# Two stacked graph layers on one core: the order of the weight loads, the place of the bias products, and when the second graph's values are made

## The chip, the cores and the metric

One core of one Trainium2 chip runs the whole program. The metric is the device time of one execution in microseconds (us). Medians of separate sets are given with the number of runs. Instruction times come from one profiled execution of each kernel; the span of a profile is about 1.8 us below the time of that same execution.

## The reference, cut to what matters

64 graphs of 256 nodes and 256 features pass two layers. All arithmetic is fp32.

```python
# layer 0: two graph attention (GAT) steps, then a feed-forward (FF) block
h = gat(gat(x, adj, W1, a1), adj, W2, a2)
h = layernorm(x + h, g_ln1, b_ln1)
x = layernorm(h + relu(h @ w_ff1 + b_ff1) @ w_ff2 + b_ff2, g_ln2, b_ln2)
# layer 1: relational attention of 8 heads, then an FF block with gelu
q, k = x @ Wq + bq, x @ Wk + bk
out = sum over r of (softmax(q k') * (adj == r)) @ (x @ Wv[r] + bv[r])
x = layernorm(x + out @ Wo + bo, g1, beta1)
x = layernorm(x + gelu(x @ W1 + b1) @ W2 + b2, g2, beta2)
```

All biases of the test inputs are zero; the kernels compute with them all the same.

## The kernel before

Graphs go in 32 pairs. Each pair is a generator of steps ("way"), and up to three ways run interleaved, so that TensorE (PE) has work of one pair while another waits.

The biases b_ff2, bo and b2 would have to be added to rows of 256 columns. The kernel adds each to the beta of the layer norm ahead of it instead, and corrects the next layer's bias for it by a tiny product: bias - W' b. These are products with a single moving column. Before any pair starts, a setup block makes them all:

```python
loaded = {0: load(0)}                     # xT, adjT, x of pair 0: first in the queue
...                                       # W1T, a2, W2, a1c; then w12 = W1 @ [W2, ...] on PE
ln = ...                                  # eight rows for the layer norms
ff0, wq, wk, wo, wv, bq, bk, bv, ff1 = ...  # all weights
with tc.tile_pool(name="psetup", bufs=2, space=PSUM) as psetup:
    for n, (name, readers) in enumerate((("L0_gnn_b_ff2", ((ff0[0], ff0[1]),)),
                                         ("L1_gnn_bo", ((wq, bq), (wk, bk))),
                                         ("L1_gnn_b2", ((ff1[0], ff1[1]),)))):
        ...                               # loads the bias row and the bias column here
        for w, bias in readers:
            pw = psetup.tile([P, 512], F32, name="pw")
            for m in range(w.shape[-1] // P):
                for c in range(KC):
                    nc.tensor.matmul(pw[:, m:m + 1], lhsT=w[:, c, m * P:(m + 1) * P], rhs=b[:, c:c + 1], ...)
            nc.vector.tensor_tensor(bias, bias, pw[:, :of], ALU.subtract)
        ...                               # for bo also one wide product with wv
psum = tc.tile_pool(name="psum", bufs=8, space=PSUM)   # the banks that the pairs' products go to
```

A pair's way, and the attention loop in it (two graphs b, two groups c of four heads each):

```python
def whole_way(pair):
    yield from gat_layers(pair, xT, adjT, x)   # inside: loaded[pair + 1] = load(pair + 1)
    yield from feed_forward(x, ff0, AF.Relu, ln[1])
    yield from attention(x, pair, adjT)
    yield from feed_forward(x, ff1, AF.Gelu, ln[3])
    ...                                        # store

for n, (b, c) in enumerate(groups):            # in attention
    ...                                        # scores of the next group, products of this one
    if (b, c) == (0, KC - 1):                  # behind the second group: values of graph 1
        v = values_tile()
        for jc in range(2):
            values(v, jc, N + jc * P, yT)
            yield 1.72, 0.0, None
```

xT has a single buffer, adjT and x have four. An fp32 product is two instructions on PE: the 8 products of a pair's first step are x16 in the trace. The second half of the printed kernel, any_inputs, is a general version behind a check of the inputs; no line shown here is from it.

Of the kernel before, what the change touches and what calls it, by code (L numbers as in the profile page):

```python
# [10 lines left out]
F32 = mybir.dt.float32  # L11
# [4 lines left out]
ALU = mybir.AluOpType  # L16
AX = mybir.AxisListType

P = 128
# [10 lines left out]
def two_layers(ctx: ExitStack, tc: tile.TileContext, t: dict, out: bass.AP, flag: bass.AP):  # L30
# [9 lines left out]
    nc = tc.nc  # L40
    B, N, D = out.shape
    NPAIR = B // 2
    KC = D // P
# [6 lines left out]
    SCALE = 1.0 / math.sqrt(DH)  # L50
    assert N == 256 and D == 256 and R == 4

    const = ctx.enter_context(tc.tile_pool(name="const", bufs=1))
    io = ctx.enter_context(tc.tile_pool(name="io", bufs=1))

    def load(pair):
        rows = slice(2 * pair, 2 * pair + 2)
        xT = io.tile([P, KC, 512], F32, name="xT")
        nc.sync.dma_start(xT, t["xT"][pair].rearrange("(c p) b n -> p c (b n)", p=P))
        adjT = io.tile([P, 4, N], I32, name="adjT", bufs=4)  # L60
        nc.sync.dma_start(adjT, t["adjT"][rows].rearrange("b (c p) n -> p (b c) n", p=P))
        x = io.tile([P, 4, D], F32, name="x", bufs=4)
        nc.sync.dma_start(x, t["x"][rows].rearrange("b (c p) d -> p (b c) d", p=P))
        return xT, adjT, x

    loaded = {0: load(0)}


    ident = const.tile([P, P], F32, name="ident")
    make_identity(nc, ident)  # L70
# [10 lines left out]
    def weights(name, pool=const):  # L81
        w = t[name]
        kc, m = w.shape[0] // P, w.shape[1]
        s = pool.tile([P, kc, m], F32, name="w_" + name)
        nc.sync.dma_start(s, w.rearrange("(c p) m -> p c m", p=P))
        return s

    def on_all(name, n, pool=const):

        v = t[name]  # L90
        s = pool.tile([P, n], F32, name="b_" + name)
        nc.sync.dma_start(s, bass.AP(tensor=v.tensor, offset=v.offset, ap=[[0, P], [1, n]]))
        return s

    def column(name):

        s = const.tile([P, t[name].shape[1]], F32, name="c_" + name)
        nc.sync.dma_start(s, t[name])
        return s
# [4 lines left out]
    with tc.tile_pool(name="setup", bufs=1) as setup, \  # L104
            tc.tile_pool(name="psetup", bufs=2, space=bass.MemoryType.PSUM) as psetup:
        w1T, a2 = weights("L0_gnn_W1T", setup), on_all("L0_gnn_a2", 2 * D, setup)
        right = setup.tile([P, KC, D + 4], F32, name="right")
        nc.sync.dma_start(right[:, :, :D], t["L0_gnn_W2"].rearrange("(c p) m -> p c m", p=P))
        nc.sync.dma_start(right[:, :, D + 2:], t["L0_gnn_a1c"])
        junk = setup.tile([P, D], F32, name="junk")  # L110
        for s in range(2):
            for c in range(KC):
                nc.vector.scalar_tensor_tensor(
                    junk, right[:, c, :D], 1.0, a2[:, s * D:(s + 1) * D], op0=ALU.mult, op1=ALU.mult,
                    accum_out=right[:, c, D + s:D + s + 1])
        for m in range(KC):
            pw = psetup.tile([P, 512], F32, name="pw")
            for c in range(KC):
                nc.tensor.matmul(pw[:, :D + 4], lhsT=w1T[:, c, m * P:(m + 1) * P], rhs=right[:, c],
                                 start=c == 0, stop=c == KC - 1)  # L120
            nc.vector.tensor_copy(w12[:, m], pw[:, :D + 4])


    ln = [tuple(on_all(n, D) for n in names) for names in (
        ("L0_gnn_g_ln1", "L0_gnn_b_ln1"), ("L0_gnn_g_ln2", "L0_gnn_b_ln2"),
        ("L1_gnn_g1", "L1_gnn_beta1"), ("L1_gnn_g2", "L1_gnn_beta2"))]
    ff0 = (weights("L0_gnn_w_ff1"), column("L0_gnn_b_ff1"), weights("L0_gnn_w_ff2"))
    wq, wk, wo = weights("L1_gnn_Wq"), weights("L1_gnn_Wk"), weights("L1_gnn_Wo")
    wv = const.tile([P, KC, 2, D], F32, name="wv")
    for c in range(KC):  # L130
        nc.sync.dma_start(wv[:, c], t["L1_gnn_Wv"][:2, c * P:(c + 1) * P, :].rearrange("r p m -> p r m"))
        nc.vector.tensor_tensor(wv[:, c, 1], wv[:, c, 1], wv[:, c, 0], ALU.subtract)
    bq, bk, bv = column("L1_gnn_bq"), column("L1_gnn_bk"), on_all("L1_gnn_bv", 2 * D)
    nc.vector.tensor_tensor(bv[:, D:], bv[:, D:], bv[:, :D], ALU.subtract)
    ff1 = (weights("L1_gnn_W1"), column("L1_gnn_b1"), weights("L1_gnn_W2"))
    bqs = const.tile([P, KC], F32, name="bqs")
    with tc.tile_pool(name="setup", bufs=1) as setup, \
            tc.tile_pool(name="psetup", bufs=2, space=bass.MemoryType.PSUM) as psetup:
        for n, (name, readers) in enumerate((("L0_gnn_b_ff2", ((ff0[0], ff0[1]),)),
                                             ("L1_gnn_bo", ((wq, bq), (wk, bk))),  # L140
                                             ("L1_gnn_b2", ((ff1[0], ff1[1]),)))):
            beta = ln[n][1]
            nc.vector.tensor_tensor(beta, beta, on_all(name, D, setup), ALU.add)
            b = setup.tile([P, KC], F32, name="c_" + name)
            nc.sync.dma_start(b, t[name + "c"])
            for w, bias in readers:
                pw = psetup.tile([P, 512], F32, name="pw")
                of = w.shape[-1] // P
                for m in range(of):
                    for c in range(KC):  # L150
                        nc.tensor.matmul(pw[:, m:m + 1], lhsT=w[:, c, m * P:(m + 1) * P], rhs=b[:, c:c + 1],
                                         start=c == 0, stop=c == KC - 1)
                nc.vector.tensor_tensor(bias, bias, pw[:, :of], ALU.subtract)
            if name == "L1_gnn_bo":
                pw = psetup.tile([P, 512], F32, name="pw")
                for c in range(KC):
                    nc.tensor.matmul(pw, lhsT=b[:, c:c + 1].to_broadcast([P, P]),
                                     rhs=wv[:, c].rearrange("p r m -> p (r m)"), start=c == 0, stop=c == KC - 1)
                nc.vector.tensor_tensor(bv, bv, pw, ALU.subtract)
        nc.vector.tensor_scalar(bqs, bq, SCALE, None, ALU.mult)  # L160

    work = ctx.enter_context(tc.tile_pool(name="work", bufs=1))
    small = ctx.enter_context(tc.tile_pool(name="small", bufs=6))
# [1 line left out]

    def bank():
        return psum.tile([P, 512], F32, name="ps")



# [119 lines left out]
        nc.vector.tensor_tensor(rows, p, rows, ALU.add)  # L290

    def layernorm(r, gb, b):
        g, beta = gb
        st, mv = small.tile([P, 2, 6], F32, name="st"), small.tile([P, 2, 2], F32, name="mv")
        rstd = small.tile([P, 2], F32, name="rstd")
        for j in range(2):
            nc.vector.bn_stats(st[:, j, :], r[:, 2 * b + j, :])  # L297
            nc.vector.bn_aggr(mv[:, j, :], st[:, j, :])
        nc.vector.tensor_scalar(rstd, mv[:, :, 1], EPS, None, ALU.add)  # L299
        nc.gpsimd.tensor_tensor(rstd, rstd, mhalf[:, :2], ALU.pow)  # L300
        for j in range(2):
            row = r[:, 2 * b + j, :]
            nc.vector.scalar_tensor_tensor(row, row, mv[:, j, 0:1], g, op0=ALU.subtract, op1=ALU.mult)
        for j in range(2):
            row = r[:, 2 * b + j, :]
            nc.vector.scalar_tensor_tensor(row, row, rstd[:, j:j + 1], beta, op0=ALU.mult, op1=ALU.add)
# [58 lines left out]
    def attention(y, pair, adjT):  # L365
# [5 lines left out]
        def values_tile():  # L371
            return work.tile([P, 2, 2 * D], F32, name="v", bufs=2)
# [71 lines left out]
        for n, (b, c) in enumerate(groups):  # L444
            last = n == len(groups) - 1
            if not last:
                ahead = scores(*groups[n + 1])
            po = bank()
            sums(e, po)
            products(c, 0, v, e, po)  # L450
            products(c, 1, v, ms, po)
            if not last:
                e, ms = ahead, of_relation_1(groups[n + 1][0], ahead)
            divided(b, c, po)
            yield 3.1 if last else 4.1, 4.8 if last else 0.8, None
            if (b, c) == (0, KC - 1):
                v = values_tile()
                for jc in range(2):
                    values(v, jc, N + jc * P, yT)
                    yield 1.72, 0.0, None  # L460
            if n == 2:
                into_rows(0)
                yield 1.75, 0.0, None
# [4 lines left out]
    def whole_way(pair):  # L468
        yield 0.0, 0.0, "gat"
        xT, adjT, x = loaded.pop(pair)  # L470
        yield from gat_layers(pair, xT, adjT, x)
        yield from feed_forward(x, ff0, AF.Relu, ln[1])
        yield 3.44, 6.0, None
        yield from attention(x, pair, adjT)
        yield from feed_forward(x, ff1, AF.Gelu, ln[3])
        nc.sync.dma_start(out[2 * pair:2 * pair + 2].rearrange("b (c p) d -> p (b c) d", p=P), x)
        yield 3.44, 0.0, None
# [442 lines left out]
```

## Time and profile before

| | before |
|---|---|
| median of the 3 runs at hand for the prediction | 3408.89 us (3407.56 to 3410.56) |
| profiled span | 3408.2 us |
| PE busy | 3341.0 us |
| PE idle (span less busy) | 67.2 us |
| first product of pair 0 | 54.67 us |

In the page's first part the busy share says which engine can be the bound, and the span less its busy time says how much a change can win without taking work off it. The prediction below shows the lines.

The product that starts a pair is the one with 260 columns in gat_layers (L251 in the kernel before, L253 in the changed one). The tiny products are L151 and L157 before; after the change the one-column ones are L157 and the wide one L167.

### The profile page before, as it was taken

To read this page: it belongs to the slowest core of one execution; us is meant where nothing else is said; L and a number is where in the kernel's file an instruction comes from. 1 tells how busy PE (TensorE), PEld (TensorE's weight loads), DVE (VectorE), ACT (ScalarE), POOL (GpSimd) and SP (SyncE) were. 2 spreads that over 40 slices of the span, in tenths; PEclk is the share of its full clock that TensorE was granted. 3 is DMA by queue.
4 is the path that set the end of the run, shared out by engine and by line. 5 is a ranking of instruction groups with operands and counts; after the bars stand their busy time and mean duration, and the time that the engine had idled before them with its cause. 6 is when DMAs were issued, how large, how long until landed. Compare 5 with 4: busy or idle time off the path is not lost.

```text
span 3408.2 us, 46925 instructions
## 1 busy us (share of the span) xinstructions
PE 3341.0 (98%) x18782; PEld 2172.0 (64%) x18782; DVE 1864.6 (55%) x4833; ACT 1366.7 (40%) x2576; POOL 202.9 (6%) x262
## 2 busy tenths in 40 slices
PE   5999999999999999999999999999999999999998
PEld 4666765675576667656756766676576567666755
DVE  3565465645645655656456556556564565565454
ACT  1424523443353255234433532552344335325432
POOL 0000000000000000000000000000000000000000
PEclk7999999999999999999999999999999999999999
DMA  5000100010010001000100100010011001000000
GB/s 162 7 13 25 38 7 7 27 36 7 13 38 19 13 26 38 7 7 30 33 7 13 38 19 13 26 37 7 7 32 31 7 13 38 19 7 19 13 1 14
DMA packets 67297, 78.19 MB, mean 23 GB/s; under 512 B 3713, under 2 KB 58113, under 8 KB 67073
## 3 DMA queue, kind: packets, MB, share of 16 engines
q1 hardware_dynamic: 67072, 75.13, 7.2%
q8 instruction: 150, 2.46, 0.3%
q14 instruction: 75, 0.61, 0.1%
HBM read 58.34 MB, written 16.78 MB: 22 GB/s over the span
## 4 chain that ended last, share of the span: by engine, by line
PE 94%; ACT 4%; DMA 1%; DVE 0%; SPq 0%; issue 0%; POOL 0%; POOLq 0%; DVEq 0%
PE ps L339 26%; PE ps L328 24%; PE ps L362 7%; PE ps L408 6%; PE ps L355 6%; PE ps L380 4%; PE ps L401 4%; PE ps L251 3%; PE ps L425 3%; PE ps L277 3%; PE ps L315 2%; PE ps L265 2%; ACT L213 2%; PE ps L223 1%; ACT L331 1%; ACT xw L267 1%
## 5 line engine op out<-in xcount | busy, mean ns | idle before, releaser
L317 ACT ACTIVATE yT<-ps 128x512 f32<-128x512 f32 x192 | 113.0, 589 | 1057.5 <-PE ps L315 1057.4
L328 PE MATMUL ps<-yT,w_L_gnn_w_ff 128*128 128x512 f32 x1024 | 478.3, 599 | 0.7 <-ACT yT L317 0.7
L328 PE MATMUL ps<-yT,w_L_gnn_W 128*128 128x512 f32 x1024 | 472.5, 596 | 1.4 <-ACT yT L317 1.4
L339 PE MATMUL ps<-w_L_gnn_w_ff,ff 128*128 128x256 f32 x2048 | 456.9, 381 | 0.0
L339 PE MATMUL ps<-w_L_gnn_W,ff 128*128 128x256 f32 x2048 | 456.8, 380 | 0.0
L339 PEld LDWEIGHTS ps<-w_L_gnn_W,ff 128*128 128x128 f32 x2048 | 389.1, 190 | 64.9 <-issue 14.6
L339 PEld LDWEIGHTS ps<-w_L_gnn_w_ff,ff 128*128 128x128 f32 x2048 | 388.0, 190 | 64.5 <-issue 14.3
L394 DVE TENSOR_TENSOR m<-a,adjT 128x512 f32<-128x512 f32 x512 | 327.5, 688 | 175.3 <-ACT a L385 131.1
L300 POOL TENSOR_TENSOR rstd<-rstd,mhalf 128x2 f32<-128x2 f32 x256 | 202.2, 790 | 3198.7 <-DVE rstd L299 3185.0
L385 ACT ACTIVATE a<-ps 128x512 f32<-128x512 f32 x512 | 264.3, 603 | 232.9 <-PE ps L380 232.7
L357 DVE TENSOR_TENSOR v<-ps,b_L_gnn_bv 128x512 f32<-128x512 f32 x128 | 88.2, 689 | 461.4 <-PE ps L355 461.4
L290 DVE TENSOR_TENSOR x<-ps,x 128x512 f32<-128x512 f32 x256 | 176.1, 688 | 262.6 <-PE ps L339 138.9
L331 ACT ACTIVATE ff<-ps,c_L_gnn_b_ff 128x512 f32<-128x512 f32 x256 | 175.9, 687 | 343.2 <-PE ps L328 343.2
L328 PEld LDWEIGHTS ps<-yT,w_L_gnn_W 128*128 128x128 f32 x1024 | 185.6, 190 | 178.7 <-issue 173.5
L328 PEld LDWEIGHTS ps<-yT,w_L_gnn_w_ff 128*128 128x128 f32 x1024 | 182.0, 190 | 177.8 <-issue 175.1
L355 PE MATMUL ps<-wv,yT 128*128 128x512 f32 x512 | 235.4, 592 | 0.0
L331 ACT ACTIVATE ff<-ps,c_L_gnn_b 128x512 f32<-128x512 f32 x256 | 175.7, 686 | 148.3 <-PE ps L328 146.7
L414 DVE RECIPROCAL s<-ps 128x256 f32<-128x256 f32 x128 | 224.2, 1751 | 0.0
L230 DVE SCALAR_TENSOR_TENSOR e<-ps,ratio,up 128x256 f32<-128x256 f32 x256 | 115.9, 477 | 172.6 <-ACT up L225 172.6
L297 DVE BATCH_NORM_STATS2 st<-x 128x6 f32<-128x256 f32 x512 | 192.8, 419 | 8.7
L355 PEld LDWEIGHTS ps<-wv,yT 128*128 128x128 f32 x512 | 97.5, 190 | 122.2 <-issue 122.2
L209 DVE TENSOR_REDUCE steep<-xw 128x1 f32<-128x4 f32 x128 | 19.8, 155 | 254.8 <-ACT xw L267 207.7
(96 smaller groups left out, 4047.9 us busy)
## 6 DMA issues: line engine op xcount, KB each, us to landing
xT<-in_xT SPq DMA_DIRECT2D x32, 512.0 KB, 4.5
adjT<-in_adjT SPq DMA_DIRECT2D x32, 512.0 KB, 3.8
x<-in_x SPq DMA_DIRECT2D x32, 512.0 KB, 4.2
out<-x SPq DMA_DIRECT2D x32, 512.0 KB, 3.2
w_L_gnn_w_ff<-in_L_gnn_w_ff SPq DMA_DIRECT2D x2, 1024.0 KB, 10.4
w_L_gnn_W<-in_L_gnn_W SPq DMA_DIRECT2D x2, 1024.0 KB, 6.9
wv<-in_L_gnn_Wv SPq DMA_DIRECT2D x2, 256.0 KB, 7.4
w_L_gnn_W1T<-in_L_gnn_W1T SPq DMA_DIRECT2D x1, 256.0 KB, 6.1
```

Source lines behind the costliest of these rows:

```text
L290: nc.vector.tensor_tensor(rows, p, rows, ALU.add)
L297: nc.vector.bn_stats(st[:, j, :], r[:, 2 * b + j, :])
L300: nc.gpsimd.tensor_tensor(rstd, rstd, mhalf[:, :2], ALU.pow)
L328: nc.tensor.matmul(p1, lhsT=w1[:, c, m * P:(m + 1) * P], rhs=yT[:, c, :], start=c == 0, stop=c == KC - 1)
L331: nc.scalar.activation(h, p1, func, bias=b1[:, m:m + 1])
L339: nc.tensor.matmul(p2[:, j * D:(j + 1) * D], lhsT=f[m][:, k * P:(k + 1) * P], rhs=w2[:, m, :], start=m == 0, stop=m == NF - 1)
L355: nc.tensor.matmul(ps, lhsT=yT[:, c, at:at + P], rhs=wv[:, c].rearrange("p r m -> p (r m)"), start=c == 0, stop=c == KC - 1)
L362: nc.tensor.matmul(ps, lhsT=w[:, d, c * P:(c + 1) * P], rhs=yT[:, d, :], start=d == 0, stop=d == KC - 1)
L385: nc.scalar.activation(a, ps[o], AF.Exp)
L394: nc.vector.tensor_tensor(m, a, adj, ALU.mult)
L408: nc.tensor.matmul(po[o * DH:(o + 1) * DH, :N], lhsT=v[:, jc, at:at + DH], rhs=ms[o][:, jc * N:(jc + 1) * N], start=r == 0 and jc == 0, st ...
L414: nc.vector.reciprocal(s, po[:, N:])
```

## The change

The intent: pair 0 should start as soon as its own data are in. Three parts: the loads are issued in the order in which they are needed; the tiny products leave the setup block and stand in pair 0's way, each ahead of the step that reads its bias; and the second graph's values move from behind the second head group to behind the first. The core of the diff, with cuts:

```diff
-    loaded = {0: load(0)}
     ...                                  # W1T, a2, W2, a1c and w12
+    loaded = {0: load(0)}
+    ln = [layernorm_weights("L0_gnn_g_ln1", "L0_gnn_b_ln1", "L0_gnn_b_ff2")]
     ff0 = (weights("L0_gnn_w_ff1"), column("L0_gnn_b_ff1"), weights("L0_gnn_w_ff2"))
+    ln.append(layernorm_weights("L0_gnn_g_ln2", "L0_gnn_b_ln2", "L1_gnn_bo"))
     ...                                  # wq, wk, wv, bq, bk, bv, wo, ln[2], ff1, ln[3]
-    with tc.tile_pool(name="psetup", ...) as psetup:
-        ...                              # all tiny products
+    def relieve(bias, w, more):          # the same products, out of a bank of the main pool
+        ...
     def whole_way(pair):
         yield from gat_layers(pair, xT, adjT, x)
+        if pair == 0:
+            relieve(ff0[1], ff0[0], ln[0][2])
         yield from feed_forward(x, ff0, AF.Relu, ln[1])
+        if pair == 0:
+            relieve_attention(ln[1][2])
         yield from attention(x, pair, adjT)
+        if pair == 0:
+            relieve(ff1[1], ff1[0], ln[2][2])
         yield from feed_forward(x, ff1, AF.Gelu, ln[3])
     # in attention
-            if (b, c) == (0, KC - 1):
-                v = values_tile()
+            if n == 0:
+                following = values_tile()
                 for jc in range(2):
-                    values(v, jc, N + jc * P, yT)
+                    values(following, jc, N + jc * P, yT)
                     yield 1.72, 0.0, None
+            if n == 1:
+                v = following
```

More of the change, by code (lines that the diff above doesn't have):

```diff
@@ L121, in two_layers, with layernorm_weights @@
             nc.vector.tensor_copy(w12[:, m], pw[:, :D + 4])
-    ln = [tuple(on_all(n, D) for n in names) for names in (
-        ("L0_gnn_g_ln1", "L0_gnn_b_ln1"), ("L0_gnn_g_ln2", "L0_gnn_b_ln2"),
-        ("L1_gnn_g1", "L1_gnn_beta1"), ("L1_gnn_g2", "L1_gnn_beta2"))]
+    loaded = {0: load(0)}
+    def layernorm_weights(g, beta, more=None):
+        return on_all(g, D), on_all(beta, D), more and (on_all(more, D), column(more + "c"))
+    ln = [layernorm_weights("L0_gnn_g_ln1", "L0_gnn_b_ln1", "L0_gnn_b_ff2")]
     ff0 = (weights("L0_gnn_w_ff1"), column("L0_gnn_b_ff1"), weights("L0_gnn_w_ff2"))
-    wq, wk, wo = weights("L1_gnn_Wq"), weights("L1_gnn_Wk"), weights("L1_gnn_Wo")
+    ln.append(layernorm_weights("L0_gnn_g_ln2", "L0_gnn_b_ln2", "L1_gnn_bo"))
+    wq, wk = weights("L1_gnn_Wq"), weights("L1_gnn_Wk")
     wv = const.tile([P, KC, 2, D], F32, name="wv")
@@ L133, in two_layers @@
     bq, bk, bv = column("L1_gnn_bq"), column("L1_gnn_bk"), on_all("L1_gnn_bv", 2 * D)
+    bqs = const.tile([P, KC], F32, name="bqs")
     nc.vector.tensor_tensor(bv[:, D:], bv[:, D:], bv[:, :D], ALU.subtract)
+    wo = weights("L1_gnn_Wo")
+    ln.append(layernorm_weights("L1_gnn_g1", "L1_gnn_beta1", "L1_gnn_b2"))
     ff1 = (weights("L1_gnn_W1"), column("L1_gnn_b1"), weights("L1_gnn_W2"))
-    bqs = const.tile([P, KC], F32, name="bqs")
-    with tc.tile_pool(name="setup", bufs=1) as setup, \
-            tc.tile_pool(name="psetup", bufs=2, space=bass.MemoryType.PSUM) as psetup:
-        for n, (name, readers) in enumerate((("L0_gnn_b_ff2", ((ff0[0], ff0[1]),)),
-                                             ("L1_gnn_bo", ((wq, bq), (wk, bk))),
-                                             ("L1_gnn_b2", ((ff1[0], ff1[1]),)))):
-            beta = ln[n][1]
-            nc.vector.tensor_tensor(beta, beta, on_all(name, D, setup), ALU.add)
-            b = setup.tile([P, KC], F32, name="c_" + name)
-            nc.sync.dma_start(b, t[name + "c"])
-            for w, bias in readers:
-                pw = psetup.tile([P, 512], F32, name="pw")
-                of = w.shape[-1] // P
-                for m in range(of):
-                    for c in range(KC):
-                        nc.tensor.matmul(pw[:, m:m + 1], lhsT=w[:, c, m * P:(m + 1) * P], rhs=b[:, c:c + 1],
-                                         start=c == 0, stop=c == KC - 1)
-                nc.vector.tensor_tensor(bias, bias, pw[:, :of], ALU.subtract)
-            if name == "L1_gnn_bo":
-                pw = psetup.tile([P, 512], F32, name="pw")
-                for c in range(KC):
-                    nc.tensor.matmul(pw, lhsT=b[:, c:c + 1].to_broadcast([P, P]),
-                                     rhs=wv[:, c].rearrange("p r m -> p (r m)"), start=c == 0, stop=c == KC - 1)
-                nc.vector.tensor_tensor(bv, bv, pw, ALU.subtract)
-        nc.vector.tensor_scalar(bqs, bq, SCALE, None, ALU.mult)
+    ln.append(layernorm_weights("L1_gnn_g2", "L1_gnn_beta2"))
+    for gbm in ln[:3]:
+        nc.vector.tensor_tensor(gbm[1], gbm[1], gbm[2][0], ALU.add)
     work = ctx.enter_context(tc.tile_pool(name="work", bufs=1))
@@ L167, in bank, with relieve_attention @@
         return psum.tile([P, 512], F32, name="ps")
+    def relieve(bias, w, more):
+        p = bank()
+        of = w.shape[-1] // P
+        for m in range(of):
+            for c in range(KC):
+                nc.tensor.matmul(p[:, m:m + 1], lhsT=w[:, c, m * P:(m + 1) * P], rhs=more[1][:, c:c + 1],
+                                 start=c == 0, stop=c == KC - 1)
+        nc.vector.tensor_tensor(bias, bias, p[:, :of], ALU.subtract)
+    def relieve_attention(more):
+        relieve(bq, wq, more)
+        relieve(bk, wk, more)
+        nc.vector.tensor_scalar(bqs, bq, SCALE, None, ALU.mult)
+        p = bank()
+        for c in range(KC):
+            nc.tensor.matmul(p, lhsT=more[1][:, c:c + 1].to_broadcast([P, P]),
+                             rhs=wv[:, c].rearrange("p r m -> p (r m)"), start=c == 0, stop=c == KC - 1)
+        nc.vector.tensor_tensor(bv, bv, p, ALU.subtract)
     alone = {}
@@ L292, in layernorm @@
     def layernorm(r, gb, b):
-        g, beta = gb
+        g, beta, _ = gb
         st, mv = small.tile([P, 2, 6], F32, name="st"), small.tile([P, 2, 2], F32, name="mv")
```

## The prediction

> **What bounds the kernel now.** I read the page's head first, then TensorE's waits after the first 100 us, then the start in windows, the chain of waits and the timeline.
>
> The page:
>
> ```profile
> span 3408.2 us, 46925 instructions
> ## 1 busy us (share of the span) xinstructions
> PE 3341.0 (98%) x18782; PEld 2172.0 (64%) x18782; DVE 1864.6 (55%) x4833; ACT 1366.7 (40%) x2576; POOL 202.9 (6%) x262
> ```
>
> TensorE (PE) is busy for all but 67.2 us of the span. A change that takes no work off PE can win at most a part of these 67 us (2.0%). Where are they? The waits of PE from 100 us to the end:
>
> ```profile
> PE ps L223 <- ACT rise L213: 18.3, 20, 0.9
> PE ps L328 <- ACT yT L317: 1.4, 2, 0.7
> ```
>
> So from 100 us on, PE waits 19.7 us: 20 times for the small exponentials ahead of a GAT broadcast. After its last FF product at about 3399 come 8 us of layer norm and store. About 39 us of idle are left, all before 100 us. The windows of the start (columns: span; PE, PEld, DVE, ACT, POOL busy; granted clock; DMA share; GB/s):
>
> ```profile
> 0.00:11.41 11.41, 0.00 (x0) 0.00 (x0) 2.86 (x12) 0.00 (x0) 0.70 (x6) 1.00 0.85 250
> 11.41:14.91 3.50, 3.50 (x8) 2.49 (x8) 0.84 (x3) 0.00 (x0) 0.00 (x0) 1.00 0.70 138
> 14.91:33.81 18.90, 0.00 (x2) 0.03 (x1) 2.01 (x5) 0.00 (x0) 0.00 (x0) 0.58 1.02 335
> 33.81:54.67 20.86, 20.61 (x84) 18.46 (x84) 3.38 (x12) 0.00 (x0) 0.00 (x0) 0.50 0.46 148
> 54.67:85.66 30.99, 23.10 (x97) 17.93 (x97) 18.05 (x64) 15.83 (x47) 1.73 (x2) 0.88 0.12 34
> ```
>
> PE idles 11.41 us, makes the product W1·W2 in 3.5, idles 18.9 while DMA runs full, then does only the tiny bias products for 20.86 us at half clock. The first pair starts at 54.67. The chain of waits shows the same:
>
> ```profile
> 3.35 6.53 DMA right<-in_L_gnn_W
> ...
> 27.73 6.09 DMA b_L_gnn_bo<-in_L_gnn_bo
> 33.81 10.37 PE pw L151 x48
> 44.18 3.62 PE pw L157 x4
> 47.80 6.63 PE pw L151 x32
> 54.67 5.82 PE ps L251 x16
> ```
>
> The tiny products wait for a bias row loaded late (L151 at 33.81). Pair 0's first product (L251) waits for the last of them, since the main PSUM pool opens only when the setup pool's banks are released. Its own inputs (w12 copied by 15.38, adjT in at 6.07) were ready some 39 us earlier.
>
> **What the Trainium skill says.** (1) "TensorE: Matmul & The Clock Gate", Part 1: The HAM clock gate: the array runs at half clock until about one busy window of 3.4 us, and falls back after an idle one. The trace agrees for full products and not for tiny ones: the granted clock was 0.50 all through 33.81 to 54.67 with PE busy 20.61 of 20.86 us, and reached 1.00 by 60, some 4 to 5 us after L251 began. (2) Same page, "LDWEIGHTS": the load costs by its 128 columns, so a product with one moving column costs a weight load. The trace agrees: 32 such took 6.8 us, 0.21 us each at half clock, while 128x128 transposes (L315, four in 0.44 us at full clock) take 0.11. (3) "DMA: Bandwidth & Descriptors", "Queues, rings and completion order": each DMA engine consumes its ring in order. So loads put first land first; the trace agrees: W2, issued at 3.35 with 2 MB ahead of it, landed at 9.88, and adjT, with 0.5 MB ahead, by 6.07.
>
> **The change, part by part.**
>
> *Loads in the order of need.* W1T, a2, W2 and a1c (0.75 MB) go first, then pair 0's xT, adjT, x (1.5 MB). adjT was in at 6.07 as the second 0.5 MB (1 MB through the queue), W2 at 9.88 after 2.25 MB: (9.88 - 6.07) / 1.25 MB = 3.05 us per MB. 0.75 MB then is in at about 6.07 - 0.25 x 3.05 = 5.3. From W2's landing to the first product took 11.41 - 9.88 = 1.53 us (DVE's a-products), now to 6.8; from it to w12's second copy 15.38 - 11.41 = 3.97 us, now to 10.8. xT (1.25 MB) is in by 6.8. So pair 0 can start at about 10.8, not 54.67: **-43.9 us**.
>
> *The tiny products in pair 0's way.* None is removed: 32 + 16 + 4 wide + 32, 20.6 us at half clock. They now follow GAT products, so the clock may be full: 20.6 / 2 = **+10.3 us** on PE. Part of it fits into pair 0's own gaps: 54.67 to 85.66 had 30.99 - 23.10 = 7.9 us of PE idle (2.9 before L265, 2.6 before L277, 1.2 around the transposes). DVE's order in this kernel shows that instructions get moved forward when ready (pair 0's adjacency reduction ran before the earlier-written setup work), so I count 4 us as filled: **-4**. They might instead pull the clock down, as one-column products did not raise it: two blocks of 3.5 us, about one half-clock window lost: **+2**.
>
> *Pair 1's xT.* It needs pair 0's buffer, free after L251, and now has to follow some 9 MB of weights. All 12.3 MB of the start took until about 43 us, so 3 MB of it were later pairs' adj and x; the weights end near 34. Pair 1's first product stood at 77.95, 23.3 after the start, so it would want xT at 34; it gets it between 36 and 44 depending on the queue's order. PE is in order, but tiny products or pair 0's FF may stand in front. I put **+3 us**.
>
> *Values behind the first head group.* The same eight products per pair (1.72 us a pair of steps' half), moved by one group. PE has no wait at the scores or the head products after 100 us, only at L223. So **0**, plus or minus a few of the 0.9 us waits, since the interleaving of the three pairs shifts.
>
> Vector additions of biases onto beta are the same three, off PE's way. Sum: -43.9 + 10.3 - 4 + 2 + 3 = -32.6. Time 3408.9 - 32.6 = **3376 us**.
>
> **Rivals.** (a) *DMA takes the place of the wait*: pair 1's xT, or a vector reduction of a later pair's adjacency placed in DVE's order before pair 0's work, comes after 9 MB and stalls pair 0 too. For: DMA is at a share of 1.0 to 43 us whatever the order, and the queue's wait for the buffer already was 23.9 us once. Against: those waits did not stop PE before, and pair 0 alone needs only 2.25 MB early. It gives back up to 15 us: 3388. (b) *Nothing hides and the clock stays low*: the tiny products cost their whole 20.6 us again. For: 20 us of them left the clock at 0.50. Against: full products stand around them. 3409 - 43.9 + 20.6 + 3 = 3389. (c) *All hidden*: the tiny products fill pair 0's gaps whole, pair 1 is not late: -43.9 + 3: 3368. (d) *The moved values change the steady state*: if 20 waits became 0 or 40, 18 us either way; the waits come from GAT steps next to FF steps, not from attention, so I give this little.
>
> **Range and chances.** The gain of the start is firm within 2 us; the tiny products vary by 10, DMA by 10, the waits by 5. Together about 11 us either side: 3376, range 3365 to 3389. 2% is 68 us, more than all of PE's idle time; slower would need PE work that the diff does not add. Faster 0.01, within 0.98, slower 0.01.
>
> **What would show it.** First L119 near 6.8 us and first L251 near 11 instead of 54.67; no PE wait of 18.9 us; the tiny products at about 0.11 us each with the granted clock at 1.00 (if 0.21 at 0.50, rival b); no PE wait before pair 1's first L251, with xT landed by then (if longer than 5 us, rival a); PE's waits after 100 us again about 20 at L223 and nothing at the head products; PE busy lower by about 10 us, all of it from the half-clock tiny products. I would be wrong if pair 0's later DVE or PE work sits behind a load that lands after 40 us, or if the count of L223's waits changes by over ten.

## The result, and the profile after

The changed kernel took 3386.78 us, the median of 6 runs (3384.74 to 3388.54); before, 3407.59 us in 6 runs (3406.43 to 3410.56). The ratio is 0.9937 with a 95% interval of 0.9924 to 0.995. A ratio here is the mean time of one kernel's runs over that of the other's runs of the same rounds, so not quite the quotient of the medians. It is a gain of 0.6%, clear of the noise and within 2%.

The head of the changed kernel's page:

```profile
span 3384.7 us, 46922 instructions
PE 3335.3 (99%) x18782; PEld 2161.4 (64%) x18782; DVE 1863.3 (55%) x4833; ACT 1366.4 (40%) x2576; POOL 202.8 (6%) x262
```

The same 18782 product instructions run. PE's idle time went from 67.2 to 3384.7 - 3335.3 = 49.4 us, and its busy time fell by 5.7 us. Together that is the 23.5 us of the spans. The medians are only 20.8 us apart: the profiled execution of the kernel before took 3409.98 us, 2.4 above the median of its six runs, that of the changed kernel 3386.56.

PE's waits from 100 us to the end of the changed kernel (total us, times, longest):

```profile
PE ps L225 <- ACT rise L215: 18.4, 20, 0.9
PE ps L330 <- ACT yT L319: 1.4, 2, 0.7
```

Nothing happened there: the same 20 waits, the same sum. The whole difference is in the start, and the waits of PE in the first 100 us (the four longest) name what is new:

```profile
PE pw L117 <- DVE junk L111: 7.3, 1, 7.3
PE ps L253 <- DMA xT<-in_xT: 5.1, 1, 5.1
PE ps L279 <- ACT xw L238: 3.3, 1, 3.3
PE ps L267 <- ACT xw L238: 2.6, 1, 2.6
```

The 18.9 us wait for a bias row is gone. In its place stands a wait of 5.1 us for pair 1's xT. The chain of waits shows how late that load was issued (start, duration, what; SPq is the queue that issues the loads):

```profile
26.84 3.57 SPq L90
...
31.01 7.51 DMA xT<-in_xT
```

The load goes out at 31.01, behind the last weight, and takes 7.51 us to land. Now PE's own timeline (start, duration, engine, line, operation, operands, count, idle before). In the kernel before, pair 1's first product and pair 0's first FF products:

```profile
77.95 3.67 PE L251 MATMUL ps<-w,xT 128*128 128x260 f32 x16
...
85.66 1.99 PE L328 MATMUL ps<-yT,w_L_gnn_w_ff 128*128 128x512 f32 x4 [0.69 <-ACT yT L317]
```

In the changed kernel, from pair 1's first product on:

```profile
38.56 5.38 PE L253 MATMUL ps<-w,xT 128*128 128x260 f32 x16 [5.10 <-DMA xT<-in_xT]
...
45.25 3.68 PE L157 MATMUL ps<-c_L_gnn_b_ff2c,w_L_gnn_w_ff 128*128 128x1 f32 x32
48.79 1.95 PE L317 MATMUL ps<-ident,x 128*128 128x128 f32 x8
51.43 3.78 PE L330 MATMUL ps<-yT,w_L_gnn_w_ff 128*128 128x512 f32 x4 [0.69 <-ACT yT L319]
55.00 2.16 PE L267 MATMUL ps<-xw,e 128*128 128x258 f32 x8
57.00 1.88 PE L330 MATMUL ps<-yT,w_L_gnn_w_ff 128*128 128x512 f32 x4
```

Compare the two L330 lines: four instructions of the same shape take 3.78 us at 51.43 and 1.88 at 57.00, and those at 51.43 took 1.99 in the kernel before. The windows of the changed kernel over the first tiny block, what follows it, the last tiny block and what follows that (window and length; busy time of PE, of its weight loads PEld, of DVE, ACT and POOL; granted clock, DMA share, GB/s) give the reason:

```profile
45.25:48.79 3.54, 3.54 (x34) 3.54 (x33) 3.34 (x13) 0.39 (x2) 0.00 (x0) 0.99 0.87 297
48.79:54.70 5.91, 5.22 (x13) 3.06 (x14) 1.52 (x4) 1.99 (x4) 0.00 (x0) 0.50 0.01 1
164.61:168.10 3.49, 3.49 (x33) 3.49 (x32) 0.88 (x2) 0.00 (x0) 0.31 (x1) 1.00 0.00 0
168.10:173.70 5.60, 5.60 (x22) 4.73 (x22) 0.16 (x1) 0.60 (x1) 0.00 (x0) 0.70 0.00 0
```

The tiny products themselves run at full clock, 3.5 us for 32 instructions. But half clock follows behind both of these blocks, although PE was busy all through them. Behind attention's block, 16 one-column and four wide instructions from 105.40 to 108.90, the clock stayed at 1.00.

From these landmarks the account of the 23.5 us can be written down. Each row is the time of a landmark after, less that of before, minus the same difference at the landmark above:

| up to | before, us | after, us | difference | step |
|---|---|---|---|---|
| pair 0's first product | 54.67 | 11.70 | -43.0 | -43.0 |
| pair 1's first product | 77.95 | 38.56 | -39.4 | +3.6: the wait for xT (5.1) and 0.7 more ahead of the last GAT products, less a faster clock in pair 0's GAT |
| pair 0's first FF product | 85.66 | 51.43 | -34.2 | +5.2: the first tiny block 3.5, and pair 1's products at half clock after the wait 1.7 |
| pair 0's second FF product group | 89.22 | 57.00 | -32.2 | +2.0: half clock behind the tiny block |
| pair 0's attention transposes | 137.62 | 108.90 | -28.7 | +3.5: attention's tiny and wide products |
| a later FF product group, behind the last tiny block | 197.66 | 174.14 | -23.5 | +5.2: the last tiny block 3.5, half clock behind it 1.7 |
| the end | 3408.2 | 3384.7 | -23.5 | 0 |

So 43.0 us were won at the start and 19.5 given back within some 160 us of pair 0's start: 10.5 for the tiny products, 3.7 for the half clock behind two blocks, 5.3 around pair 1's xT.

### The profile page after: what moved, and what is told of

The parts are those of the page before. It is cut to its first block, busy times and chain, and to the rows that moved or that the text cites. A ratio compares the mean times of both kernels' runs of the same rounds, so it can differ in the third digit from the quotient of the medians.

```text
span 3384.7 us, 46922 instructions
## 1 busy us (share of the span) xinstructions
PE 3335.3 (99%) x18782; PEld 2161.4 (64%) x18782; DVE 1863.3 (55%) x4833; ACT 1366.4 (40%) x2576; POOL 202.8 (6%) x262
## 4 chain that ended last, share of the span: by engine, by line
PE 95%; ACT 4%; DMA 1%; SPq 0%; issue 0%; DVE 0%; POOL 0%; POOLq 0%; DVEq 0%
PE ps L341 26%; PE ps L330 25%; PE ps L364 7%; PE ps L410 7%; PE ps L357 6%; PE ps L382 4%; PE ps L403 4%; PE ps L253 3%; PE ps L427 3%; PE ps L279 3%; PE ps L317 3%; PE ps L267 2%; ACT L215 2%; PE ps L225 1%; ACT L333 1%; ACT xw L269 1%
## 5 line engine op out<-in xcount | busy, mean ns | idle before, releaser
L330 PE MATMUL ps<-yT,w_L_gnn_w_ff 128*128 128x512 f32 x1024 | 480.0, 601 | 0.7 <-ACT yT L319 0.7
L330 PE MATMUL ps<-yT,w_L_gnn_W 128*128 128x512 f32 x1024 | 472.4, 596 | 1.4 <-ACT yT L319 1.4
L341 PEld LDWEIGHTS ps<-w_L_gnn_W,ff 128*128 128x128 f32 x2048 | 388.2, 190 | 65.8 <-issue 14.6
L330 PEld LDWEIGHTS ps<-yT,w_L_gnn_W 128*128 128x128 f32 x1024 | 185.3, 190 | 179.0 <-issue 173.7
L330 PEld LDWEIGHTS ps<-yT,w_L_gnn_w_ff 128*128 128x128 f32 x1024 | 182.1, 190 | 178.9 <-issue 175.9
## 6 DMA issues: line engine op xcount, KB each, us to landing
w_L_gnn_W<-in_L_gnn_W SPq DMA_DIRECT2D x2, 1024.0 KB, 10.3
```

The costliest lines, as they stand in the source:

```text
L330: nc.tensor.matmul(p1, lhsT=w1[:, c, m * P:(m + 1) * P], rhs=yT[:, c, :], start=c == 0, stop=c == KC - 1)
L341: nc.tensor.matmul(p2[:, j * D:(j + 1) * D], lhsT=f[m][:, k * P:(k + 1) * P], rhs=w2[:, m, :], start=m == 0, stop=m == NF - 1)
```

## The experiments

All ten kernels gave a correct result. Times are medians of 4 runs (6 where said) with the ratio to the kernel before of the same rounds; that one took 3410.45 to 3410.97 us (median of 7 or 8 runs) in these sets.

| run | median, us | ratio to before | 95% interval |
|---|---|---|---|
| loads_only | 3396.56 | 0.9959 | 0.9943 to 0.9976 |
| inway_only | 3384.45 | 0.9923 | 0.9907 to 0.994 |
| no_tiny | 3370.86 | 0.9883 | 0.9867 to 0.99 |
| no_values_move | 3386.86 | 0.9932 | 0.9915 to 0.9948 |
| xt_early | 3383.38 | 0.992 | 0.9903 to 0.9936 |
| tiny_in_gaps | 3374.4 | 0.9893 | 0.9877 to 0.991 |
| ff1_spread | 3384.06 | 0.9921 | 0.9904 to 0.9938 |
| best | 3376.08 | 0.9898 | 0.9882 to 0.9915 |
| gaps_and_spread | 3374.14 | 0.9893 | 0.9876 to 0.9909 |
| after_again (6 runs) | 3385.05 | 0.9926 | 0.9912 to 0.994 |

### The three parts one by one

**loads_only.** The new order of loads with the old setup block:

```diff
 # the changed kernel, without its three relieve calls and with the values as before
+    with tc.tile_pool(name="psetup2", bufs=2, space=PSUM) as psetup:
+        ...                  # all tiny products, ahead of the pairs
```

> The new order of loads alone; the tiny products stay together in a setup block ahead of pair 0, the values where they were. My theory (pair 0 waits for the whole setup block, not for its own data): the last tiny block now waits for the second FF's W1, in at about 33 us, then costs 6.9 us at half clock, so pair 0's first product stands at about 41 us instead of 54.67: about 3394 us (14 less than before). Rival (the order of loads is the main gain): within 3 us of the changed kernel, 3387. In both the 18.9 us wait of TensorE gets shorter.

It took 3396.56 us, 14 less than before. Pair 0's first product stood at 40.09 us. Of PE's waits in its first 100 us, the two at the tiny products:

```profile
PE pw L152 <- DMA w_L_gnn_w_ff<-in_L_gnn_w_ff: 4.7, 1, 4.7
PE pw L152 <- DMA w_L_gnn_W<-in_L_gnn_W: 3.0, 1, 3.0
```

The first and the last block now wait for their own weights instead of a late bias row; the setup block still ends only after the last of the large weights. This is my theory's number (3394), not the rival's (3387).

**inway_only.** The other part alone:

```diff
 # the kernel before: loads in its order
-    with tc.tile_pool(name="psetup", ...) as psetup:
-        ...                  # all tiny products
+    more = [(on_all(n, D), column(n + "c")) for n in ("L0_gnn_b_ff2", "L1_gnn_bo", "L1_gnn_b2")]
     def whole_way(pair):
+        if pair == 0:
+            relieve(...)     # the three calls, as in the change
```

> The tiny products in pair 0's way alone; loads in the old order, values where they were. My theory: pair 0's first product stands at about 15.5 us (w12 was copied by 15.38 in the kernel before), 39 us earlier; the tiny products cost 10.5 us at full clock and the half clock after two of their blocks 3.7; pair 1's xT, which made TensorE wait 5.1 us in the changed kernel, comes in at about the same time, but is asked for 4 us later, so the wait shrinks to about 1: about 3383 to 3387, the whole gain without the new order of loads. Rival (order of loads matters): pair 0's later loads hold it up, 3395 or more.

It took 3384.45 us, as fast as the whole change. Two lines of its timeline say why the order of loads adds nothing that these runs resolve:

```profile
16.22 5.83 PE L250 MATMUL ps<-w,xT 128*128 128x260 f32 x16 [0.52 <-DVE w L121]
...
39.20 3.67 PE L250 MATMUL ps<-w,xT 128*128 128x260 f32 x16
```

Pair 0 starts at 16.22, 4.5 us later than in the changed kernel, but pair 1 starts at 39.20 with no wait, 0.6 us later than there. The 4.5 us that the new order wins at pair 0 are lost again waiting for pair 1's xT, which comes behind all weights in both: it was in at 38.5 there, and here at 37.6 (issued at 31.41, 6.2 us to landing).

**no_values_move.** The changed kernel with the values back:

```diff
-            if n == 0:
-                following = values_tile()
+            if (b, c) == (0, KC - 1):
+                v = values_tile()
                 ...
-            if n == 1:
-                v = following
```

> The changed kernel with the second graph's values back behind the second head group. My theory: no difference, 3386.8 within 2 us; TensorE's waits after 100 us again 20 at the broadcast's transposes. Rival (the moved values carry part of the gain or of the give-back): 5 us or more either way.

It took 3386.86 us, and its profiled span is 3384.7, the same as with the moved values; after 100 us PE waits 18.4 us in 20 waits at the broadcast's transposes, as before. The moved values are worth nothing here.

### What the tiny products cost

**no_tiny.** The products are left out, which is right only because the biases are zero:

```diff
         if pair == 0:
-            relieve(ff0[1], ff0[0], ln[0][2])        # and the third call likewise
+            nc.vector.tensor_scalar(bqs, bq, SCALE, None, ALU.mult)   # in place of the second
```

> The changed kernel without the tiny products (right only since these inputs' biases are zero, done on purpose). My theory: they cost their 10.5 us and 3.7 us of half clock behind two blocks, all exposed: about 3372 to 3373, 14 less than the changed kernel. Rival (they stand beside waits that would be there anyway, the give-back is DMA): less than 4 us less, 3383 or more.

It took 3370.86 us, 16 less than the 3386.8 that the changed kernel took in another set of rounds; by the ratios 0.9937 - 0.9883 = 0.0054 of 3410, 18 us, with an uncertainty of some 8 us; against after_again, on the same chip, it is 14.2. The profiled spans differ by 13.4 us, close to the 10.5 + 3.7 of the account. The clock behind the place of the first block is the sharper witness; the first FF product group in this kernel:

```profile
48.72 1.98 PE L330 MATMUL ps<-yT,w_L_gnn_w_ff 128*128 128x512 f32 x4 [0.74 <-ACT yT L319]
```

1.98 us, not 3.78: without the block the clock stays up. The rival that the tiny products stand beside other waits is refuted.

**ff1_spread.** Is it the unbroken block that pulls the clock down? The last 32 tiny instructions are handed out, four behind each step of pair 0's first FF (relieve_one is relieve for one m):

```diff
             f.append(h)
+            if spread:                                   # pair 0, first FF
+                relieve_one(ff1[1], ff1[0], ln[2][2], m)
             yield 1.72, 0.0, None
 # and the third relieve call is dropped
```

> The changed kernel with the second FF's 32 tiny instructions handed out four at a time behind the steps of pair 0's first FF. My theory: the half clock behind a block comes from the block, an unbroken 3.5 us of one-column products; spread out, they keep the clock at 1.00 and the 1.7 us lost in the FF product behind the block goes: 3385, and at 160 to 175 us the clock stays 1.00. Rival (the clock fell for another reason): the same half clock at that place.

From 165 to 170 us the changed kernel and this one read (PE busy, clock, DMA share, GB/s):

```profile
165.00:170.00 5.00, 5.00 (x37) 0.82 0.00 0
```

```profile
165.00:170.00 5.00, 5.00 (x25) 1.00 0.00 0
```

The clock stays at 1.00 where no block stands, so the block was the cause there. The other profiles agree at both places. The four instructions of pair 0's first FF group took 3.40 to 3.78 us in the six profiles with the block ahead of them and 1.98 or 1.99 in the six without; the sixteen FF products behind the last block's place took 4.79 to 6.03 us in the five profiles with that block and 3.62 in each of the seven without. Each group of four costs about 0.36 us (L164 at 61.24, the next product at 61.60), so the spread products still cost 3 us. The time, 3384.06, is not distinguishable from the changed kernel's; the profiled span, 3385.1, is even 0.4 longer: this execution happened to take some 1 us more before the first FF, and half clock behind the first block reached further (the L274 products at 56.78 took 2.90 us, where L267 took 2.16 in the changed kernel). The gain of 1.7 us is below what these runs resolve.

### Hiding what is given back

**xt_early.** Pair 1's loads come right behind the first FF's weights, and xT has two buffers:

```diff
-        xT = io.tile([P, KC, 512], F32, name="xT")
+        xT = io.tile([P, KC, 512], F32, name="xT", bufs=2)
     ff0 = (...)
+    loaded[1] = load(1)
```

> The changed kernel with two buffers for xT and pair 1's loads right after the first FF's weights. My theory: the 5.1 us wait of TensorE for pair 1's xT goes, and with it the half clock in the product behind it; net about 5 us of the time, 3381 to 3382. Rival (the transposes and FF of pair 0 are held by the vector engine's layer norm, so an earlier pair 1 only waits later): less than 2 us.

It took 3383.38 us. The wait for xT is gone from its profile and the span, 3380.9, is 3.8 us shorter, a little under the 5 expected: in this execution the clock was halved during pair 0's first sixteen graph attention products (L268 there, L267 in the changed kernel), which took 6.63 us instead of 3.75. By the times alone, ratio 0.992 against 0.9937 and 0.9926, it is a gain inside the noise; on the same chip (after_again, below) it is 1.7 us. The trace shows the wait gone with no other in its place, as the theory has it, but the size isn't settled, and the rival's "less than 2 us" is not excluded.

**tiny_in_gaps.** The first block goes ahead of pair 0's last GAT products, the others ahead of pair 1's first product:

```diff
             e.append(gat_weights(z, D, *a.pop(0), adjT, empty, b))
             yield 0.5, b * 4.4, None
+        if pair == 0:
+            relieve(ff0[1], ff0[0], ln[0][2])
         ...                                    # the last GAT products
+        if pair == 0:
+            relieve_attention(ln[1][2])
+            relieve(ff1[1], ff1[0], ln[2][2])
         done_with("gat")
```

> The changed kernel with the first FF's tiny products ahead of pair 0's last GAT products (TensorE waits 3.3 us there) and all others ahead of pair 1's first product (it waits 5.1 us for xT there). My theory: they then cost only what does not fit: the first block 0 to 0.5 us, the others 7 us in a gap of 5 if at full clock (gain 10 us or more, 3374 to 3377), 14 us if the gap before has halved the clock (gain 4 to 6 us, 3381 to 3383). Rival (a block costs its 3.5 us wherever it stands): no gain.

It took 3374.4 us, some 11 us less than the changed kernel. Its timeline:

```profile
26.22 3.63 PE L157 MATMUL ps<-c_L_gnn_b_ff2c,w_L_gnn_w_ff 128*128 128x1 f32 x32
29.71 5.39 PE L281 MATMUL ps<-xw,e 128*128 128x256 f32 x16
34.94 0.95 PE L157 MATMUL ps<-c_L_gnn_boc,w_L_gnn_Wq 128*128 128x1 f32 x8
35.75 1.03 PE L157 MATMUL ps<-c_L_gnn_boc,w_L_gnn_Wk 128*128 128x1 f32 x8
36.64 1.96 PE L167 MATMUL ps<-wv,c_L_gnn_boc 128*128 128x512 f32 x4
38.44 4.41 PE L157 MATMUL ps<-c_L_gnn_b2c,w_L_gnn_W 128*128 128x1 f32 x32
42.72 6.31 PE L253 MATMUL ps<-w,xT 128*128 128x260 f32 x16
```

No idle time stands ahead of any of these lines: the blocks fill the 3.3 us wait and the 5.1 us wait of the changed kernel. Only the last block and the half clock in the product behind it (6.31 us) stick out. The sixteen products behind the first block (L281) took 5.39 us, as long as behind the idle gap in the changed kernel (L279 at 28.05, 5.41): the block fills the wait, but here the clock was lowered behind it just as behind idle time.

**best.** Pair 1's early loads, the first block in the GAT gap, the last one spread out (the edits of xt_early, the first half of tiny_in_gaps and ff1_spread together):

> Pair 1's early loads with two xT buffers, the first FF's tiny products in pair 0's GAT gap, the second FF's spread out, attention's as in the changed kernel. My theory: 5 us for xT, 3.5 + 2 for the first block and the half clock behind it, 1.7 for the second: 3386.8 - 12 = about 3375, under both kernels. Rival (the gains overlap, since pair 0's layer norm then ends the wait in any case): about 3380.

3376.08 us, near the expected sum (3375), and below both kernels. The interval of its ratio reaches from 3370 to 3381 us, so the rival's 3380 is not excluded, and a part of what the rival names is in the trace. A wait for pair 0's layer norm, which the profiles of the changed kernel don't have, stands ahead of the transposes:

```profile
PE ps L327 <- DVE x L318: 1.4, 1, 1.4
```

**gaps_and_spread.** The first two blocks in the gaps, the last spread out, loads as in the change:

```diff
 # the first half of tiny_in_gaps, relieve_attention as there, and ff1_spread
-            relieve(ff1[1], ff1[0], ln[2][2])  # not ahead of pair 1
```

> The changed kernel with the first FF's tiny products in pair 0's GAT gap, attention's ahead of pair 1's first product (3.5 us in the 5 us wait for xT), the second FF's spread out behind the steps of the first FF. My theory: against the run with all in the gaps, the second FF's block no longer stands ahead of pair 1 (4.3 us there and 2.6 of half clock behind it) and costs about 3 us spread out: 3374.4 - 4 = about 3370 to 3371. Rival (the [...]clock window decides and the gains do not add): 3374 to 3376, as the two runs before it.

3374.14 us: the time is the rival's, not mine. The profiled span did shrink, from 3374.6 to 3372.3, and the block's 4.41 us and the 6.31 are gone from the trace, but pair 0 happened to start at 12.57 instead of 11.63. Of the three hidden variants none is shown faster than another.

**after_again.** The changed kernel in the same rounds as the last run:

> The changed kernel as it is, in the same rounds, for a comparison on one chip: 3385 to 3388, and by profile again a 5 us wait for pair 1's xT, 20 waits at the broadcast's transposes, and half clock behind two blocks of tiny products.

3385.05 us in 6 runs; the profiled span was 3384.5. Its profile repeats the first one: 5.3 us of wait for pair 1's xT, the 20 waits (18.4 us), and a clock of 0.50 from 49 to 55. It is the comparison on one chip: 3374.14 against 3385.05 is 11 us less, and the intervals of their ratios do not overlap.

## Why the prediction was right or wrong

The time, 3386.8, lies in the range, 11 us above the predicted 3376, and the gain is below 2%, as forecast. It lies at the edge: the "11 us either side" end at 3387, and only the printed range goes on to 3389. By its own terms:

- **The early start, -43.9 us.** Measured -43.0. The 0.9 us between: W2 was in some 0.5 us later than the 5.3 worked out (the vector engine's first use of it is at 5.92), and the product W1·W2 took 3.84 us instead of 3.50, so that the second copy of w12 came later behind its start. Pair 0's adjacency reduction, which ran between the two copies, was not needed for this: in inway_only it did not stand there, and the product took 3.84 us too. inway_only shows that the term belongs to the tiny products' leaving the setup block; on top of that move the load order supplies 4.5 us of the start. (Alone, with the setup block in place, it brought pair 0 forward by 14.6 us in loads_only: the two parts do not add.)
- **The tiny products at full clock, +10.3.** Measured 10.5.
- **Hidden in pair 0's gaps, -4.** Measured 0. This is the step that failed: the overlap of the tiny products with pair 0's gaps. I read from the vector engine's order that instructions are moved forward when ready and carried that over to PE, although the prediction itself says, of pair 1's xT, that PE is in order. PE ran them where they were written: L157 at 45.25, behind pair 1's GAT products, with the gaps of 2.6 and 3.3 us open earlier. tiny_in_gaps shows that the 3.3 us gap does hold the first block, if it is written there.
- **The clock, +2.** Measured 3.7. The cause was right; but it happens behind both long blocks, 2.0 and 1.7 us, where I counted one.
- **Pair 1's xT, +3.** Measured 5.3 with the half clock behind the wait, less what pair 0's GAT won by a faster clock. The landing at 38.5 lies within the predicted 36 to 44; the wait of 5.1 us just passes the 5 us that the prediction set as the sign of rival (a). (The "9 MB of weights" ahead of it are all earlier loads; 1.5 MB of them are pair 0's own.) What I missed is its relation to the first term: a 4.5 us earlier pair 0 asks for xT 4.5 us earlier, and so the wait returns the load order's gain. inway_only shows it, with no wait at all.
- **The moved values, 0.** Measured 0, with the same 20 waits.

The sum of the last-named terms was +11.3 and is +19.5; 4 of the 8 us are the hiding that did not come, 1.7 the second clock loss and 2.3 xT. Of the rivals, (a) was present at a third of the size I gave it, (b) was wrong in its clock during the blocks (0.11 us each, as predicted) and right that nothing hides; (c) and (d) did not occur. I predicted PE's busy time to fall by 10 us; it fell by 5.7, since products at half clock count as busy for twice as long, after the wait and behind the blocks.

What stays open is the place of the clock windows in a single execution. Pair 0's first product took 3.77 us in some profiles and 5.8 to 6.0 in others with the same instructions ahead of it in the different kernels, so a profile may be 2 us longer or shorter for this reason alone, and differences of that size between two profiles are not explained here.

## What to carry to other kernels

When one engine is nearly always busy, the account of its idle time by stage bounds a change before it is built: here 67 us in all, some 39 of them in the first 100 us. Busy time at half clock has to be counted beside it: 20.6 us of tiny products, which took 10.5 at full clock. A setup block that a PSUM pool or another resource separates from the main work delays everything by its last load; put its pieces where they are read, and better still write them into a place where the engine is known to wait. Re-ordering loads pays only up to the next load that somebody waits for, so follow the queue past the first consumer.

## What the Trainium skill lacked or had wrong

- "TensorE: Matmul & The Clock Gate", Part 1: The HAM clock gate, ties the clock to how busy PE was in the last window. The runs show that being busy in the profile's sense is not enough: 20.61 us of products, most with one moving column, left the clock at 0.50 in the kernel before (33.81 to 54.67), and a 3.5 us block of them at full clock was followed by half clock (0.50 from 48.79 to 54.70) with no idle PE ahead of it; the last block's products, spread out in fours, kept it at 1.00. No section says this of one-column products.
- The same page, "LDWEIGHTS", gives a weight load's time by its columns without the clock. One-column fp32 instructions, whose weight loads fill their block (PEld busy 6.90 us beside PE's 6.96 in the kernel before, both 3.54 in the changed kernel), took 0.21 us each at half clock and 0.11 at full clock.
- The same page warns that records of the clock can't be trusted one by one. A case to add: the granted clock reads 1.00 in the first 15 us of both kernels, while in the kernel before its first eight 260-column instructions took 3.5 us, 0.44 each, and pair 1's sixteen of the same width 3.67 us, 0.23 each, at full clock.
- "DMA: Bandwidth & Descriptors", "Queues, rings and completion order", says that rings are consumed in order, but not what that does to a load that is needed soon: pair 1's 0.5 MB were issued at 31.01 us behind some 9 MB of earlier loads, landed 7.51 us later (the median of such loads in this kernel is 4.6), and cost PE 5.1 us. The share of the late issue and that of the slow landing were not measured apart.
